# Layer 3 of a four-layer graph network: the second half of the attention score as one more projection column

## The chip, the cores and the metric

The kernel runs on one core of a Trainium2 chip. The metric is the device time of one execution in microseconds. Before the change it was 2033.64 us, the median of three runs (2031.97 to 2036.11).

A core has five engines that work side by side, each on its own stream of instructions: TensorE (PE in the profile; its weight loads are PEld), VectorE (DVE), ScalarE (ACT), GpSimd (POOL) and SyncE (SP), which here issues DMAs. They meet at semaphores.

## What is computed

Four graph layers with residual connections run on 128 graphs of 64 nodes with 256 features. The change lies in the last one, a graph attention:

```python
def _L3_gnn_ref(h, adj_matrix, W, a):
    Wh = jnp.einsum('bnf,fo->bno', h, W)
    a1, a2 = (a[:Fout, 0], a[Fout:, 0])
    s1 = Wh @ a1
    s2 = Wh @ a2
    e = s1[:, :, None] + s2[:, None, :]
    e = jnp.where(e >= 0, e, ALPHA * e)
    e = jnp.where(adj_matrix[None] == 0, -jnp.inf, e)
    attention = jax.nn.softmax(e, axis=-1)
    h_prime = jnp.einsum('bij,bjo->bio', attention, Wh)
    return h_prime
...
h = jnp.maximum(_layernorm(x, axis=-1), 0.0)
x = x + _L3_gnn_ref(h, adj, L3_gnn_W, L3_gnn_a)
```

A score is the sum of two halves: s1 of the row's node i and s2 of the column's node j. Both are linear in the features, so s2 = h (W a2).

## The kernel before

**Tiling.** The 8192 tokens go through layer 3 in 16 chunks of 512. A chunk is four tiles of 128 tokens, and a tile holds two graphs of 64 nodes, one in partitions 0 to 63, the other in 64 to 127. Everything is in 32-bit floats; an ordinary product of TensorE appears as two instructions in the trace, a transpose as one.

**The loop.** The pass n of the loop at L2005 works on several chunks at different stages:

- `second_norm(n + 2)` (L1852): TensorE transposes `o` (the output of layer 2, scaled) back to tokens, eight transposes at L1860; VectorE adds the residual (L1865, 128x1024) and takes the statistics (L1869, L1870); from chunk 3 on GpSimd makes the root of the variance and the shift (L1879 to L1882) and the normalised `h`, four instructions at L1886.
- `scale_o(n + 4)` (L1841): GpSimd scales layer 2's output into `o`, two instructions at L1848.
- `features(n + 1)` (L1894): eight transposes of `h` (L1901), then ScalarE applies the ReLU on its way to `hT` (L1904).
- `project3(n)` (L1910): for each tile two products of `hT` with `wext`, the 256 columns of W and one column W a1, 257 columns; ScalarE copies the bank to `wh` (L1925).
- `turn(n - 1)` (L1955): four transposes of the exponentials (L1960), copied by VectorE and ScalarE into `field` (L1964).
- `dense_scores(n)` (L1927): s2 of the chunk, spread over the rows, is made on TensorE from `hT` with `wa2`, in which the vector W a2 stands 64 times; four products with 64 columns of weights. VectorE adds s1, the column 256 of `wh` (L1937), applies the leaky ReLU (L1943), adds the mask (L1944) and takes the maximum (L1946); ScalarE makes the exponentials (L1949).
- `dense_values(n - 1)` (L1968): four products of `field` with `wh` (L51, "wh,field"), which VectorE scales and adds to the residual (L1975).

**The order.** The kernel is written in this program order, and a scheduler places the instructions of each engine's stream by its own cost model, except those marked with `late`, which stay in program order. In layer 3 few are marked, so an edit can move other instructions on every engine. `bank()` takes one of four PSUM banks, `pair_bank()` one of two double banks. `mm` (L51) records every product, so the profile gives L51 for `wext`, `wa2` and `wh` alike; they are told apart by the operands.

**Tables.** `late_tables` (L188 on) fills `wext` and `wa2` in layer 0's stage, among them `eye` (the 64x64 unit matrix, twice) in a pool that is freed afterwards.

Of the kernel before, what the change touches and what calls it, by code (L numbers as in the profile page):

```python
# [9 lines left out]
F32 = mybir.dt.float32  # L10
# [4 lines left out]
ALU = mybir.AluOpType  # L15
AX = mybir.AxisListType

P = 128
T = 64
D = 256  # L20
# [11 lines left out]
def gnn_stack_kernel(ctx: ExitStack, tc: tile.TileContext, a: dict, out: bass.AP):  # L32
    nc = tc.nc
# [10 lines left out]
    def bank():  # L44
        return psums["now"].tile([P, 512], F32, tag="bank", name="bank", bufs=psums["banks"])
# [4 lines left out]
    def mm(o, lhsT, rhs, start=True, stop=True):  # L50
        nc.tensor.matmul(o, lhsT, rhs, start=start, stop=stop)  # L51
# [20 lines left out]
    def late(ins):  # L72

        tc.keep_in_program_order(ins)
# [106 lines left out]

    tab2 = ctx.enter_context(tc.tile_pool(name="tab2", bufs=1))
    bdH = tab2.tile([P, P], F32, tag="bdH", name="bdH")
    wext = tab2.tile([P, 2, D + 1], F32, tag="wext", name="wext")
    wa2 = tab2.tile([P, 2, T], F32, tag="wa2", name="wa2")
    mask3 = tab2.tile([P, T], F32, tag="mask3", name="mask3")

    def late_tables():  # L188
        with ExitStack() as setup:
            s2 = setup.enter_context(tc.tile_pool(name="s2", bufs=1, side="right"))  # L190
            nc.sync.dma_start(out=wext[:, :, :D], in_=a["W3"])
            w3T = s2.tile([P, 2, D], F32, tag="w3T", name="w3T")
            nc.sync.dma_start(out=w3T, in_=a["W3T"])
            a3 = s2.tile([P, 2, 2], F32, tag="a3", name="a3")
            nc.sync.dma_start(out=a3, in_=a["a3"])

            late(nc.vector.tensor_scalar(mask3, adj2, 0.0, NEG, ALU.is_equal, ALU.mult))
            yield

            eye = s2.tile([P, T], F32, tag="eye", name="eye")  # L200
            for h in range(2):
                r = slice(h * T, (h + 1) * T)
                nc.vector.tensor_copy(eye[r, :], ident[r, r])
            an = s2.tile([P, T], F32, tag="an", name="an")
            anT = s2.tile([P, T], F32, tag="anT", name="anT")
            nc.vector.tensor_tensor(an, adj2, eye, ALU.add)
            nc.vector.tensor_tensor(anT, adjT2, eye, ALU.add)
            yield
            deg = s2.tile([P, 3], F32, tag="deg", name="deg")
            diag = s2.tile([P, T], F32, tag="diag", name="diag")  # L210
            nc.vector.tensor_tensor(diag, an, eye, ALU.mult)
            nc.vector.tensor_reduce(deg[:, 0:1], anT, AX.X, ALU.add)
            nc.vector.tensor_reduce(deg[:, 1:2], an, AX.X, ALU.add)
            nc.vector.tensor_reduce(deg[:, 2:3], diag, AX.X, ALU.add)
            yield
            dinv = s2.tile([P, 1], F32, tag="dinv", name="dinv")
            nc.vector.tensor_tensor(dinv, deg[:, 0:1], deg[:, 1:2], ALU.add)
            nc.vector.tensor_tensor(dinv, dinv, deg[:, 2:3], ALU.subtract)
            nc.gpsimd.tensor_tensor(dinv, dinv, half_power[:, 0:1], ALU.pow)
            yield  # L220
            dinv_b = s2.tile([P, P], F32, tag="dinv_b", name="dinv_b")
            nc.vector.tensor_copy(dinv_b, dinv.to_broadcast([P, P]))
            nc.vector.memset(bdH, 0.0)
            nc.vector.tensor_scalar(anT, anT, dinv, None, ALU.mult)
            yield
            p = bank()
            mm(p[:, :T], dinv_b[:T, :], ident[:T, :T])
            yield
            for h in range(2):
                r = slice(h * T, (h + 1) * T)  # L230
                nc.vector.tensor_tensor(bdH[r, r], p[r, :T], anT[r, :], ALU.mult)
            yield

            p = bank()
            for c in range(2):
                for k in range(2):
                    mm(
                        p[:, 2 * c : 2 * c + 2],
                        w3T[:, k, c * P : (c + 1) * P],
                        a3[:, k, :],  # L240
                        k == 0,
                        k == 1,
                    )
            yield
            for c in range(2):
                nc.vector.tensor_copy(wext[:, c, D:], p[:, 2 * c : 2 * c + 1])
                nc.vector.tensor_copy(wa2[:, c, :], p[:, 2 * c + 1 : 2 * c + 2].to_broadcast([P, T]))
            yield


# [195 lines left out]
    with ExitStack() as l0:  # L446
# [39 lines left out]
        with ExitStack() as conv:  # L486
# [38 lines left out]
            for h in range(2):  # L525
                r = slice(h * T, (h + 1) * T)
# [3 lines left out]
            p = bank()  # L530
# [4 lines left out]
            def graph_convolutions(n):  # L535
# [53 lines left out]
                if n >= NCH // 2:  # L589
                    nc.sync.dma_start(out=hmem[n], in_=dst)  # L590

            tables = chain(edge_tables(), late_tables())
            under_way = []
            for n in range(NCH + 4):
# [265 lines left out]
        for slot in range(len(tasks) + 2):  # L860
# [24 lines left out]
            if new:  # L885
                next(one)
                flight.append((new, one))
                at, k = new[0], new[2]
# [6 lines left out]
                if step.w == MAX_SKIP and step.t == 2 and k < 2 and step.g < NGR - 1:  # L895
                    for u in range(2):
                        n = 4 * step.g + 2 * u + k
                        later.append((slot, "x", n))
            while later and later[0][0] <= slot:
                _, kind, n = later.pop(0)  # L900
# [27 lines left out]
    with ExitStack() as l1:  # L928
# [32 lines left out]
        for g, c in last_outs:  # L961
            for u in range(2):
                n = 4 * g + 2 * u + c
# [482 lines left out]
    with ExitStack() as l2:  # L1446
        def pool2(name, bufs):
            return l2.enter_context(tc.tile_pool(name=name, bufs=bufs, reuse_waits="tile"))
# [53 lines left out]
        with ExitStack() as dense2:  # L1502
# [67 lines left out]
            with ExitStack() as first_dense:  # L1570
# [43 lines left out]
                for slot, (pr, m2) in enumerate(tasks):  # L1614
                    n = slot + 3
# [128 lines left out]
        t4 = pool2("t4", 2)  # L1744
# [9 lines left out]
        xts, norms, hT3, att3 = {}, {}, {}, {}  # L1754
# [155 lines left out]
        def project3(n, tiles):  # L1910

            if n not in att3:
                wh = t4.tile([P, 4, D + 1], F32, tag="wh", name="wh", bufs=3)
                att3[n] = [wh, None, None]
            for i in tiles:
                p = bank()
                for k in range(2):
                    mm(
                        p[:, : D + 1],
                        hT3[n][:, k, i * P : (i + 1) * P],  # L1920
                        wext[:, k, :],
                        k == 0,
                        k == 1,
                    )
                nc.scalar.copy(att3[n][0][:, i, :], p[:, : D + 1])  # L1925

        def dense_scores(n):  # L1927

            wh, hT = att3[n][0], hT3.pop(n)

            p = bank()
            for k in range(2):
                hv = hT[:, k, :].rearrange("p (i o t) -> p o i t", o=2, t=T)
                for h in range(2):
                    mm(p[h * T : (h + 1) * T, : 4 * T], wa2[:, k, :], hv[:, h], k == 0, k == 1)
            e = t4.tile([P, 4, T], F32, tag="e3", name="e3")
            nc.vector.tensor_tensor(  # L1937
                e,
                p[:, : 4 * T].rearrange("p (i t) -> p i t", t=T),
                wh[:, :, D:].to_broadcast([P, 4, T]),  # L1940
                ALU.add,
            )
            nc.vector.scalar_tensor_tensor(e, e, 0.2, e, ALU.mult, ALU.max)  # L1943
            nc.vector.tensor_tensor(e, e, mask3.unsqueeze(1).to_broadcast([P, 4, T]), ALU.add)  # L1944
            nmx = stat.tile([P, 4], F32, tag="nmx3", name="nmx3")
            nc.vector.tensor_reduce(nmx, e, AX.X, ALU.max, negate=True)  # L1946
            den = stat.tile([P, 4], F32, tag="den3", name="den3")
            for i in range(4):
                nc.scalar.activation(  # L1949
                    e[:, i, :], e[:, i, :], AF.Exp, bias=nmx[:, i : i + 1], accum_out=den[:, i : i + 1]  # L1950
                )
            nc.vector.reciprocal(den, den)
            att3[n][1:] = [e, den]
# [45 lines left out]
        for _ in start:  # L1999
            pass  # L2000
        project3(0, (0, 1))
        for _ in second:
            pass
        scale_o(3)
        for n in range(NCH + 1):  # L2005
            if 4 <= n + 4 < NCH:
                fetch(n + 4)
            if n + 2 < NCH:
                for _ in second_norm(n + 2):
                    pass  # L2010
            if n + 4 < NCH:
                scale_o(n + 4)
            if n == 0:
                project3(0, (2, 3))
                dense_scores(0)
                features(1)
                continue
            if n + 1 < NCH:
                features(n + 1)
            if 0 <= n < NCH:  # L2020
                project3(n, (0, 1))
            if n >= 1:
                turn(n - 1)
            if 0 <= n < NCH:
                project3(n, (2, 3))
                dense_scores(n)
            if n >= 1:
                dense_values(n - 1)
# [68 lines left out]
```

## Time and profile before

| what | us |
|---|---|
| median of three runs | 2033.64 |
| the profiled execution | 2017.19 |
| its span, first to last instruction | 2015.0 |
| TensorE busy | 1963.0 |
| VectorE busy | 1245.3 |
| ScalarE busy | 1160.6 |
| GpSimd busy | 365.1 |
| products with wa2, 128 instructions | 17.3 |
| layer 3, first o transpose to the end of the span | 1860.7 to 2015.0 |

The busy times are of the profiled execution, whose own time is below the median of the other runs. Lines of a timeline give the start in us from the span's start, the busy time, the engine, the line, the operation with output and inputs, the number of instructions put together, and in brackets how long the engine had been idle and what ended that. Lines of a table by stretches give the length, then the busy time and the number of instructions of TensorE, its weight loads, VectorE, ScalarE and GpSimd, then the granted TensorE clock as a share of full speed, the DMA share and GB/s. Lines of a group give the number of instructions, their busy time and the mean of one in ns.

### The profile page before, as it was taken

Reading aid. Unit: us, or ns where it says so; the run is one execution under the profiler, and the core shown is the slowest. Engines: PE = TensorE matmul, PEld = TensorE weight load, DVE = VectorE, ACT = ScalarE, POOL = GpSimd, SP = SyncE. Lnnn points to the kernel's source line nnn. Section 1 sums busy time; section 2 is a strip of 40 time slices with the busy share of each in tenths; the row PEclk is TensorE's granted clock in tenths of the full one; section 3 lists DMA queues with packets and bytes.
Section 4 is the critical chain, followed back from the end, with each engine's and each line's share of the span. In section 5 each row is a group of like instructions: output and inputs, shape, how many; then the busy total and the mean of one; then the engine's idle time right before and its main releaser. Section 6 shows DMA issues by size and latency. Waiting matters only on the chain. (4 is left out here: it accounts for less than half of the span.)

```text
span 2015.0 us, 26089 instructions
## 1 busy us (share of the span) xinstructions
PE 1963.0 (97%) x9720; PEld 1395.9 (69%) x9720; DVE 1245.3 (62%) x2418; ACT 1160.6 (58%) x2177; POOL 365.1 (18%) x534
## 2 busy tenths in 40 slices
PE   7999999999999999999999999999999999999998
PEld 5777468866678864888666888666566875444786
DVE  8774675575475567665645655534444877886776
ACT  4343775565465547665555555577776556691544
POOL 3000031030030011310300200213223420000563
PEclk9999999999999999999999999999999999999999
DMA  8422000010010053001001000621334841022012
GB/s 289 134 76 87 0 22 1 0 42 0 1 42 1 1 189 103 21 1 42 1 0 42 1 0 25 204 92 58 126 110 141 300 147 53 0 84 84 32 63 74
DMA packets 63486, 135.62 MB, mean 67 GB/s; under 512 B 6272, under 2 KB 40960, under 8 KB 61056
## 3 DMA queue, kind: packets, MB, share of 16 engines
q1 hardware_dynamic: 57120, 109.65, 16.2%
q0 software_dynamic: 5632, 24.12, 3.2%
q8 instruction: 76, 1.25, 0.3%
q14 instruction: 50, 0.41, 0.1%
q10 hardware_dynamic: 608, 0.20, 0.0%
HBM read 87.54 MB, written 46.40 MB: 66 GB/s over the span
## 5 line engine op out<-in xcount | busy, mean ns | idle before, releaser
L719 ACT ACTIVATE gate<-gate,bias 128x256 f32<-128x256 f32 (+2 forms) x368 | 247.2, 678 | 180.6 <-DVE gate L735 99.6
L691 PE MATMUL pa<-xop,sih 128*128 128x256 f32 (+2 forms) x1056 | 342.4, 417 | 8.9 <-DVE gate L745 8.7
L691 PEld LDWEIGHTS pa<-xop,sih 128*128 128x128 f32 x1056 | 199.0, 190 | 82.9 <-issue 21.8
L691 PE MATMUL pc<-xop,wih 128*128 128x256 f32 (+2 forms) x736 | 251.1, 423 | 0.0
L735 DVE TENSOR_TENSOR gate<-pb,gate 128x256 f32<-128x256 f32 (+2 forms) x184 | 87.4, 475 | 226.5 <-PE pb L691 150.5
L691 PE MATMUL pa<-lstm_h,shh 128*128 128x256 f32 (+1 forms) x672 | 212.7, 398 | 0.0
L691 PEld LDWEIGHTS pc<-xop,wih 128*128 128x128 f32 x736 | 139.8, 190 | 51.2 <-issue 23.0
L750 DVE TENSOR_TENSOR gate<-pc,gate 128x256 f32<-128x256 f32 (+2 forms) x184 | 87.6, 476 | 112.8 <-PE pc L691 112.6
L691 PEld LDWEIGHTS pa<-lstm_h,shh 128*128 128x128 f32 x672 | 127.7, 190 | 30.2
L1057 ACT ACTIVATE lr<-pair 128x1024 f32<-128x1024 f32 x128 | 123.7, 1018 | 34.9 <-PE pair L1047 33.3
L691 PE MATMUL pc<-lstm_h,whh 128*128 128x256 f32 (+1 forms) x448 | 141.8, 398 | 0.0
L734 ACT COPY gate<-pa 128x256 f32<-128x256 f32 (+2 forms) x184 | 76.1, 413 | 95.3 <-PE pa L691 94.9
L745 DVE TENSOR_TENSOR gate<-pa,gate 128x256 f32<-128x256 f32 (+2 forms) x184 | 87.4, 475 | 43.9 <-PE pa L691 43.3
L1018 PE MATMUL bank<-wlv,hT 128*128 128x260 f32 x480 | 112.9, 387 | 0.4
L1027 DVE TENSOR_TENSOR xq<-bank,xq 128x260 fp32r<-128x260 f32 x64 | 27.1, 428 | 138.9 <-ACT xq L1026 138.9
L719 ACT ACTIVATE gate<-pa,bias 128x256 f32<-128x256 f32 (+2 forms) x184 | 93.8, 510 | 31.2 <-PE pa L691 29.8
L739 ACT COPY gate<-pa 128x256 f32<-128x256 f32 (+2 forms) x184 | 75.2, 409 | 53.1 <-PE pa L691 52.1
L1018 PEld LDWEIGHTS bank<-wlv,hT 128*128 128x128 f32 x480 | 88.5, 190 | 22.9 <-issue 9.1
L691 PE MATMUL pa<-xop,wih 128*128 128x256 f32 (+1 forms) x320 | 101.6, 399 | 2.8 <-ACT xop L672 2.7
L691 PE MATMUL pb<-xop,wih 128*128 128x256 f32 (+1 forms) x320 | 100.4, 398 | 0.0
L691 PEld LDWEIGHTS pc<-lstm_h,whh 128*128 128x128 f32 x448 | 85.1, 190 | 20.1
L742 ACT COPY gate<-pc 128x256 f32<-128x256 f32 (+2 forms) x136 | 57.9, 426 | 52.5 <-PE pc L691 51.9
(366 smaller groups left out, 3842.5 us busy)
## 6 DMA issues: line engine op xcount, KB each, us to landing
field<-keep SPq DMA_DIRECT2D x4, 2304.0 KB, 13.2
wih<-in_WihT SPq DMA_DIRECT2D x8, 1024.0 KB, 7.1
xres<-in_x SPq DMA_DIRECT2D x16, 512.0 KB, 4.6
xa<-xres POOLq DMA_DIRECT2D x16, 512.0 KB, 4.1
dense<-field POOLq DMA_DIRECT2D x4, 2048.0 KB, 10.0
xin<-xb SPq DMA_DIRECT2D x16, 512.0 KB, 3.7
h<-xb SPq DMA_DIRECT2D x16, 512.0 KB, 3.6
xin<-in_x SPq DMA_DIRECT2D x15, 512.0 KB, 5.1
```

Source lines behind the costliest of these rows:

```text
L691: ins = nc.tensor.matmul(p[:, : self.N], weights[kind, self.phase](k, q), x[k], start=first_ and kind == "ih", stop=kind == "hh" or not se ...
L719: nc.scalar.activation(out, in_, AF.Tanh if q == 2 else AF.Sigmoid, bias=bias[:, self.w - 1, 2 * q + j : 2 * q + j + 1],)
L734: nc.scalar.copy(blk[0, 0], pa[:, :N])
L735: nc.vector.tensor_tensor(blk[0, 0], pb[:, :N], blk[0, 0], ALU.add)
L739: nc.scalar.copy(blk[1, 0], pa[:, :N])
L742: (nc.vector.tensor_copy if not self.t and self.w > 1 else nc.scalar.copy)(blk[1, 1], pc[:, :N])
L745: nc.vector.tensor_tensor(blk[1, 1], pa[:, :N], blk[1, 1], ALU.add)
L750: nc.vector.tensor_tensor(blk[1, 0], pc[:, :N], blk[1, 0], ALU.add)
L1018: ins = nc.tensor.matmul(o, hTs[n][:, k, i * P : (i + 1) * P], wlv[:, k, cols], start=k == 0, stop=k == 1)
L1027: nc.vector.tensor_tensor(xq[:, 1, :], p[:, :QS], xq[:, 0, :].bitcast(F32), ALU.subtract)
L1057: nc.scalar.activation(lr, p, AF.Relu)
```

## The change

`wext` gets a second extra column, W a2, so `project3` computes s2 for each node along with the rest, in 258 columns. `dense_scores` then has s2 with one node in each partition and needs it along the row. GpSimd multiplies each s2 with a row of `eye`, which gives `across`: in row j only column j is not zero. One product with `same_graph`, which is one where both nodes are in the same graph, sums over the nodes of a graph and so writes s2 of every node j into every row. This stands in place of the four products with `wa2`. `eye` moves into a pool that stays.

```diff
-    wext = tab2.tile([P, 2, D + 1], F32, tag="wext", name="wext")
-    wa2 = tab2.tile([P, 2, T], F32, tag="wa2", name="wa2")
+    wext = tab2.tile([P, 2, D + 2], F32, tag="wext", name="wext")
+    same_graph = tab2.tile([P, P], F32, tag="same_graph", name="same_graph")
+    eye = tab2.tile([P, T], F32, tag="eye", name="eye")
...
-            eye = s2.tile([P, T], F32, tag="eye", name="eye")
+            nc.vector.memset(same_graph, 0.0)
             for h in range(2):
                 r = slice(h * T, (h + 1) * T)
                 nc.vector.tensor_copy(eye[r, :], ident[r, r])
+                nc.vector.memset(same_graph[r, r], 1.0)
...
             for c in range(2):
-                nc.vector.tensor_copy(wext[:, c, D:], p[:, 2 * c : 2 * c + 1])
-                nc.vector.tensor_copy(wa2[:, c, :], p[:, 2 * c + 1 : 2 * c + 2].to_broadcast([P, T]))
+                nc.vector.tensor_copy(wext[:, c, D:], p[:, 2 * c : 2 * c + 2])
...
-                wh = t4.tile([P, 4, D + 1], F32, tag="wh", name="wh", bufs=3)
+                wh = t4.tile([P, 4, D + 2], F32, tag="wh", name="wh", bufs=3)
...
                     mm(
-                        p[:, : D + 1],
+                        p[:, : D + 2],
                         hT3[n][:, k, i * P : (i + 1) * P],
                         wext[:, k, :],
                         k == 0,
                         k == 1,
                     )
-                nc.scalar.copy(att3[n][0][:, i, :], p[:, : D + 1])
+                nc.scalar.copy(att3[n][0][:, i, :], p[:, : D + 2])
...
         def dense_scores(n):
-            wh, hT = att3[n][0], hT3.pop(n)
-
+            wh = att3[n][0]
+            hT3.pop(n)
+            across = t4.tile([P, 4, T], F32, tag="across", name="across")
+            nc.gpsimd.tensor_tensor(
+                across,
+                wh[:, :, D + 1 :].to_broadcast([P, 4, T]),
+                eye.unsqueeze(1).to_broadcast([P, 4, T]),
+                ALU.mult,
+            )
             p = bank()
-            for k in range(2):
-                hv = hT[:, k, :].rearrange("p (i o t) -> p o i t", o=2, t=T)
-                for h in range(2):
-                    mm(p[h * T : (h + 1) * T, : 4 * T], wa2[:, k, :], hv[:, h], k == 0, k == 1)
+            mm(p[:, : 4 * T], same_graph, across.rearrange("p i t -> p (i t)"))
...
-                wh[:, :, D:].to_broadcast([P, 4, T]),
+                wh[:, :, D : D + 1].to_broadcast([P, 4, T]),
                 ALU.add,
             )
```

## The prediction

> **What bounds the kernel now.** I read the page first (which engine is full), then the stage in windows (is it full there too), then the timeline of one round (what each queue holds, and when). A round is one pass n of the loop at L2005; there are sixteen, one for each chunk of 512 tokens, and the change touches nothing else that lies on a long path.
>
> ```profile
> span 2015.0 us, 26089 instructions
> PE 1963.0 (97%) x9720; PEld 1395.9 (69%) x9720; DVE 1245.3 (62%) x2418; ACT 1160.6 (58%) x2177; POOL 365.1 (18%) x534
> ```
>
> ```profile
> 1920.00:1940.00 20.00, 20.00 (x122) 16.38 (x121) 16.33 (x45) 9.74 (x37) 14.39 (x25) 1.00 0.16 53
> ```
>
> In this stage too TensorE (first column after the stretch) is never idle, while GpSimd (the fifth) is busy 14.39 of 20 us, four times its mean share. So product time saved counts in full here, but only while nothing makes TensorE wait, and GpSimd has little room. The timeline shows where:
>
> ```profile
> 1926.49 0.23 POOL L1879 TENSOR_SCALAR ln_rs<-ln_mv 128x4 f32<-128x4 f32 x1 [2.44 <-DVE ln_mv L1870]
> 1926.86 1.08 PE L51 MATMUL bank<-hT,wa 128*64 128x256 f32 x8
> 1927.88 2.00 PE L51 MATMUL pair<-wh,field 128*128 128x256 f32 x8
> ...
> 1928.54 2.61 POOL L1886 TENSOR_SCALAR h<-h,ln_rs,ln_nm 128x256 f32<-128x256 f32 x4
> ...
> 1929.71 1.04 PE L1860 MATMUL pair<-ident,o 128*128 128x128 f32 x8
> ...
> 1931.13 1.52 POOL L1848 TENSOR_SCALAR o<-h,scale,shift 128x512 f32<-128x512 f32 x2
> ...
> 1931.76 1.21 DVE L1865 TENSOR_TENSOR h<-pair,h 128x1024 f32<-128x1024 f32 x1
> 1931.89 1.04 PE L1901 MATMUL pair<-ident,h 128*128 128x128 f32 x8
> ```
>
> The score products (hT,wa) start at 1926.86 in this round and at 1935.47 in the next, so a round is 8.61 us. GpSimd's block (root, four h tiles, two o tiles) runs from 1926.49 to 1931.13 + 1.52 = 1932.65, 6.16 us, and starts at almost the same moment as the score products. It waits 2.44 us for VectorE's statistics before it.
>
> **Removed and added on TensorE.** Per round eight wa instructions go, 1927.88 - 1926.86 = 1.02 us. The product with the graph ones is one product of 256 columns, two instructions; the four of wh,field take 1929.71 - 1927.88 = 1.83, so one takes 0.46. The extra column costs sixteen instructions x 1 of 257 columns, 0.01. Net 0.55 us a round, 8.8 in sixteen, if TensorE stays full.
>
> **Added around it.** The product now waits for a new GpSimd instruction (across), which waits for ScalarE's copy of the last tile. Its price is in no row. The nearest rows are two-input products of 128x256 on GpSimd:
>
> ```profile
> L680 POOL TENSOR_TENSOR xop<-xop 128x256 f32<-128x256 f32 x10 | 15.9, 1592 | 0.8
> ...
> L137 POOL TENSOR_TENSOR w1S<-w1T,w1S 128x256 f32<-128x256 f32 x1 | 0.7, 747 | 0.0
> ```
>
> Bounds 0.72 and 1.59 us; the lower rows are dense in shape and run beside a less loaded VectorE, so I take 0.8. From the last projection, across alone needs 0.1 + 0.37 (copy) + 0.1 + 0.8 + 0.1 = 1.5 us.
>
> **Where the queues hold it.** This decides. In the built streams of the changed kernel, across(n) stands on GpSimd behind root(n+2), four h(n+2) and two o(n+4), that is, behind the 6.16 us block that today starts with the score products; and in front of root(n+3). On TensorE the ones product of round n stands two or four wh,field products after the last projection (in every second round also half of the o transposes), and in front of the o transposes of chunk n+3, all or half. Their streams around a round of kind A, cut to these lines:
>
> ```
> GpSimd:  root(n+2) x4, h(n+2) x4, o(n+4) x2, across(n), root(n+3) ...
> TensorE: wext x4, wh,field x4, o-transposes(n+3) x4, ones product(n), o-transposes(n+3) x4, wext(n+1) ...
> VectorE: L1975, scores, L1975, L1943, L1865, L1944, statistic, maximum, statistics ...
> ```
>
> In the trace each engine's instructions come in the order of its stream, so there is a ring from one ones product to the next: o transposes(n+3) -> L1865 and statistics on VectorE -> root, h(n+3), o(n+5) on GpSimd -> across(n+1) -> ones product(n+1) -> o transposes(n+4). Today TensorE does not wait in it, since the score products need no GpSimd. What is queued behind the waiting product is the rest of wh,field and all transposes; VectorE waits for both, and GpSimd for VectorE.
>
> Length of the ring, from rows of this timeline (pace from start to start). Rounds with half of the transposes already done (A): product and handover 0.63; on VectorE scores 0.46, one L1975 0.45, L1943 0.46, then L1865 1.24, L1944 0.46, maximum 0.45, statistics 1.70 (2.01 less the field copy): 5.85. Handover 0.09, GpSimd block 6.16, handover 0.1, across 0.73, handover 0.15: 13.1 us. Rounds with all transposes and two wh,field behind the product (B): 0.63, then four L1975 (1.76), scores, L1943, L1944, maximum (1.83) stand before L1865, 1.24, then reciprocal and statistics with the field copy 2.11: 7.57, and the same 7.23: 14.8. Against 8.61.
>
> The score products of rounds 0 to 13 are thirteen intervals, 1987.12 - 1875.06 = 112.06 us. After: round 0 to 1 13.2 (as A, with a reciprocal more); five B 74.0; five A 65.4; 11 to 12 without the o tiles 14.8 - 1.52 = 13.3; 12 to 13 one wh,field less again 12.8. Sum 178.7, so +66.6. The first product waits 1.45 for its chain (+1.5); after round 13 there is no block, and what is saved there (0.55 a round) goes into the exposed chain: 0.
>
> **Corrections.** VectorE will be idle while GpSimd works, and h then costs less: 1.09 for two, 0.545 each where VectorE was idle, against 0.653: -0.43 a round, -5.6. Across at 0.8 instead of 0.73: +0.9. And the clock:
>
> ```profile
> 1858.00:1860.00 2.00, 0.00 (x0) 0.00 (x0) 1.84 (x8) 0.30 (x1) 0.00 (x0) 0.83 0.62 223
> ...
> 1870.00:1872.00 2.00, 2.00 (x7) 1.49 (x6) 0.00 (x0) 0.38 (x2) 0.00 (x0) 0.50 0.00 0
> 1872.00:1874.00 2.00, 2.00 (x12) 1.92 (x11) 0.92 (x3) 1.51 (x4) 0.87 (x2) 0.76 0.00 0
> ```
>
> At the stage's start TensorE has a gap of 4.0 us; the granted clock (third figure from the end) falls to half within it, 2.7 us in, and stays there until 1873.0, 5.8 us after TensorE became steadily busy. A round has 8.0 us of TensorE work, so the gaps will be 3 to 6 us. In a round that starts at half clock the first handover grows by 0.45, and in B the field copy, which stands before the last statistic, comes 0.85 later still: +0.45 (A), +1.3 (B), +11.8 if all thirteen rounds start so. Since a slow start fills part of the next gap I take half, +5.9.
>
> The Trainium skill, "TensorE: Matmul & The Clock Gate", Part 1, What's actually happening, puts the fall at an idle window of about 3.4 us and the recovery at about 3.4 us busy, on a free-running window. The fall here agrees roughly, the recovery at 5.8 us was slower; by the page's recovery my estimate is that the cold rounds lose about half as much, some 3 us less in the sum.
>
> Sum: 66.6 + 1.5 - 5.6 + 0.9 + 5.9 = +69.3, rounded to +70. In the profiled execution 2017.19 becomes 2087; the median of the runs lies 16.4 higher, and the difference is carried to it: 2033.64 + 70 = **2104 us**. Its own ends: no clock loss, +63 (2097); all rounds cold, h not faster and across at 1.59, 66.6 + 1.5 + 11.8 + 14 x 0.86 = +92 (2126).
>
> The tables cost nothing: two memsets of graph ones on VectorE (128x128 took 0.165 us at L65) lie before the first data arrive; bare, 0.4. wa's two copies go, 0.3 at most, in a stage that TensorE fills. No DMA is added or moved; SP's stream is the same.
>
> **Rivals.**
> - Faster, on the other side: the ones product waits only for its own chain. That would be so if GpSimd's block were done by the last projection; then 8.8 is gained less 0.6 in the B rounds (1.5 needed, 0.91 covered): -4 to -9, 2025 to 2030. For it: the saving is real and TensorE is full. Against: the block would have to start 6 us earlier than at 1926.49, and VectorE's statistics end just there. It decides once across is queued ahead of root and h. Chance 0.05.
> - No change: that gain is eaten by a later exponential, whose transposes already wait at the end (2006.02): 2030 to 2037. Chance 0.03.
> - Slower still: the clock stays at half through whole rounds. TensorE's 8.0 us become 15.8 (eight projection instructions took 3.59 at half, 1.83 at full), more than the ring: 13 x 15.8 - 112 = +93 and more, 2127 to 2140. For it: the gaps return each round. Against: each round begins with over 5.8 us of steady work. Chance 0.09.
>
> The forecast has 0.83. **Range** 2085 to 2130: the forecast's own ends, some room below for a ring shorter than rows say, and the lower edge of the third rival. Faster by over 0.2% (4 us, about what a measurement here can tell) 0.05, same 0.03, slower 0.92.
>
> **What would show it.** Right: ones products 13 to 15 us apart; TensorE idle before them with across as releaser, in total some 60 us; across starting within 0.1 us of the last o tile; the last slices of TensorE at 5 to 7 tenths, their clock under 1. Step by step: a ones product near 0.46, across near 0.8, the block 5.7 to 6.2. Wrong: across starting long before the o tiles end, rounds under 9 us, or TensorE waiting for VectorE's exponential input rather than for GpSimd.

## The result and the profile after

The changed kernel takes 2093.61 us (median of six runs, 2090.16 to 2095.92) against 2032.81 for the kernel before (six runs on the same chip): a ratio of 1.0295, 95% interval 1.028 to 1.031, so some 60 us slower. 2104 was predicted, in a range of 2085 to 2130.

The profiled execution took 2090.16. The page, its first lines, TensorE's busy slices with the granted clock, and the chain of work that ended last:

```profile
span 2088.4 us, 25890 instructions
PE 1985.4 (95%) x9624; PEld 1409.1 (67%) x9624; DVE 1238.7 (59%) x2419; ACT 1158.3 (55%) x2177; POOL 370.9 (18%) x550
...
PE   7999999999999999999999999999999999997777
...
PEclk9999999999999999999999999999999999998998
...
POOL 4%; DVE 3%; PE 1%; issue 1%; ACT 0%; DVEq 0%; POOLq 0%; ACTq 0%
```

TensorE issues 96 instructions fewer, and is busy for longer. The loss sits in the last four slices of 40, which are layer 3; the chain that sets the end now runs over GpSimd and VectorE, where that of the kernel before ran mostly over TensorE:

```profile
PE 22%; DVE 3%; ACT 1%; issue 1%; POOL 0%; POOLq 0%; DVEq 0%; ACTq 0%
```

In the 167.0 us of the thirteen intervals between the score products (a stretch of the windows view, columns as before, TensorE first, GpSimd fifth, then the clock), beside the 112.0 us of the kernel before:

```profile
1890.00:2057.00 167.00, 124.59 (x597) 97.15 (x597) 82.21 (x249) 57.53 (x201) 76.86 (x144) 0.91 0.11 38
```

```profile
1875.00:1987.00 112.00, 111.41 (x677) 89.58 (x676) 87.79 (x253) 58.74 (x201) 71.42 (x125) 1.00 0.17 57
```

TensorE was full and is now idle for 42 of 167 us. The view of waits of the changed kernel (who waited for whom, us in total, times, longest) tells what for:

```profile
POOL ln_rs L1880 <- DVE ln_mv L1871: 81.4, 12, 8.5
...
DVE e L1942 <- PE bank L51: 53.4, 13, 6.3
...
PE bank L51 <- POOL across L1933: 32.2, 14, 3.7
```

Three engines wait for one another in a circle: GpSimd's root for VectorE's statistics, VectorE's scores for TensorE's product, TensorE's product for GpSimd's across. No single share of busy time shows that. The timeline of one round shows the circle (changed kernel; line numbers are one to five above those of before):

```profile
1928.61 0.70 PE L51 MATMUL bank<-across,same_graph 128*128 128x256 f32 x2 [1.50 <-POOL across L1933]
...
1932.45 1.22 DVE L1866 TENSOR_TENSOR h<-pair,h 128x1024 f32<-128x1024 f32 x1
...
1935.54 0.16 DVE L1871 BATCH_NORM_AGGREGATE ln_mv<-ln_st 128x2 f32<-128x6 f32 x1
1935.80 0.23 POOL L1880 TENSOR_SCALAR ln_rs<-ln_mv 128x4 f32<-128x4 f32 x1 [7.25 <-DVE ln_mv L1871]
...
1937.85 2.17 POOL L1887 TENSOR_SCALAR h<-h,ln_rs,ln_nm 128x256 f32<-128x256 f32 x4
...
1940.00 1.52 POOL L1849 TENSOR_SCALAR o<-h,scale,shift 128x512 f32<-128x512 f32 x2
1941.48 0.62 POOL L1933 TENSOR_TENSOR across<-wh,eye 128x256 f32<-128x256 f32 x1
1942.15 1.22 PE L51 MATMUL bank<-across,same_graph 128*128 128x256 f32 x2 [3.61 <-POOL across L1933]
```

From 1928.61 every row waits for the one above it, VectorE's rows through its queue, which it works off from the scores at 1929.41 without a pause: 7.09 us until VectorE's last statistic ends, 0.10 of handover, 5.68 for GpSimd's block, 0.62 for across, 0.05, and the next product starts after 13.54 us. The thirteen intervals are 12.95, 13.55, 11.87, 13.54, 12.39, 13.62, 11.87, 13.63, 12.39, 13.62, 12.17, 12.13 and 13.32. Their sum is 167.05 against 112.06 before, +55.0. From the start of layer 3 (the first o transpose) to the first product +1.3, from the fourteenth product to the end +3.2: +59.5 in all, which agrees with the medians. (The spans differ by 73.4, since the profiled execution of before was quicker than its other runs; its layer 3 began 14 us earlier.)

### The profile page after: what moved, and what is told of

Same layout as the page of the kernel before. It is cut to its first block, busy times and chain, and to the rows that moved or that the text cites. A ratio compares the mean times of both kernels' runs of the same rounds, so it can differ in the third digit from the quotient of the medians.

```text
span 2088.4 us, 25890 instructions
## 1 busy us (share of the span) xinstructions
PE 1985.4 (95%) x9624; PEld 1409.1 (67%) x9624; DVE 1238.7 (59%) x2419; ACT 1158.3 (55%) x2177; POOL 370.9 (18%) x550
## 5 line engine op out<-in xcount | busy, mean ns | idle before, releaser
L1048 PE MATMUL pair<-sd_hot,xq 64*128 64x512 f32 x512 | 80.0, 428 | 7.4 <-ACT lr L1058 6.4
```

The lines of the kernel that those rows point to most:

```text
L1048: ins = nc.tensor.matmul(p[:, par, :], queries[it][r, piece, c * P : (c + 1) * P], sd_hot[r, :], start=piece == 0, stop=piece == 1,)
```

## The experiments

Each kernel was timed against the kernel before on the same chip. That kernel's own median was 2030.29, 2017.22 and 2031.04 us in the three groups of runs, so the ratios are what compares. "First" is from layer 3's first o transpose to the first score product, "loop" the thirteen intervals, "tail" the rest, all in us from the profiles.

| kernel | ratio to before, 95% | first | loop | steady round | tail |
|---|---|---|---|---|---|
| before | 1 | 14.4 | 112.1 | 8.61 | 27.9 |
| changed | 1.0295 (1.028 to 1.031) | 15.7 | 167.1 | 11.87 to 13.6 | 31.1 |
| across unread | 0.9957 (0.9943 to 0.997) | 14.5 | 103.6 | 7.84 | 26.6 |
| across ahead of the block | 1.0074 (1.005 to 1.0097) | 20.7 | 112.8 | 8.68 | 31.9 |
| across on VectorE | 1.0018 (1.0001 to 1.0034) | 15.0 | 112.0 | 8.44 | 30.6 |
| values first | 1.0256 (1.0229 to 1.0284) | 15.2 | 160.0 | 11.97 to 13.3 | 31.5 |
| changed, h doubled | 1.0331 (1.0314 to 1.0348) | 15.7 | 172.2 | 12.9 and 14.1 | 31.9 |
| before, h doubled | 1.0006 (0.9996 to 1.0016) | 13.7 | 112.1 | 8.61 | 29.9 |
| VectorE, values first | 1.0118 (1.0101 to 1.0135) | 15.0 | 131.0 | 9.92 | 32.1 |
| VectorE, split | 1.0012 (1.0003 to 1.0022) | 15.3 | 112.9 | 8.44 | 30.6 |
| o on ScalarE | 1.0299 (1.0284 to 1.0314) | 18.8 | 164.4 | 12.05 to 13.4 | 30.4 |
| VectorE, h transposes first | 0.9981 (0.9968 to 0.9993) | 14.6 | 107.5 | 8.15 | 29.3 |
| the same, split | 0.997 (0.9958 to 0.9981) | 14.8 | 104.7 | 7.84 | 27.9 |

### The wait alone taken away

```diff
-            mm(p[:, : 4 * T], same_graph, across.rearrange("p i t -> p (i t)"))
+            mm(
+                p[:, : 4 * T].rearrange("p (i t) -> p i t", t=T),
+                same_graph,
+                eye.unsqueeze(1).to_broadcast([P, 4, T]),
+            )
```

> The ones product reads the constant eye matrix (four copies side by side) in place of across, so the second score half is left out of the result. GpSimd still computes across in every round, in the same place of its order (after root, four h, two o), but nothing reads it. GpSimd does the same work as in the changed kernel; only TensorE's wait for it is gone. Ring theory (the time comes from the product waiting for across behind the block, which itself waits for what the product released): the loop is cut, rounds fall back to about 8.1 us (8.61 before less 0.55 saved on TensorE), so the time is about 2033 - 8.8 = 2024, range 2020 to 2034. Rival 'load' (0.62 us more GpSimd work per round, contention with VectorE, later h): the time stays above 2070, product intervals stay at 12 to 13.6 us. Rival 'clock' (the half clock after idle spells is most of the +61): follows the ring theory here, since the idle spells go.

Measured: 0.9957, 2021.08 against 2030.29, -9.2 us. One round of its timeline:

```profile
1934.48 0.61 POOL L1933 TENSOR_TENSOR across<-wh,eye 128x256 f32<-128x256 f32 x1
...
1936.43 0.23 POOL L1880 TENSOR_SCALAR ln_rs<-ln_mv 128x4 f32<-128x4 f32 x1 [1.33 <-DVE ln_mv L1871]
...
1936.77 0.59 PE L51 MATMUL bank<-eye,same_graph 128*128 128x256 f32 x2
1937.20 1.89 PE L51 MATMUL pair<-wh,field 128*128 128x256 f32 x8
```

GpSimd has exactly the instructions that it has in the changed kernel; the product has no bracket, so TensorE did not wait for it, and rounds are 7.84 us. Eleven of the thirteen intervals are 7.83 or 7.84. So GpSimd's added work costs nothing by itself; the price is the wait alone. (TensorE's stream moves a little with it: all four values products then follow the product in every round.)

### The queue alone changed

```diff
-                nc.gpsimd.tensor_scalar(rs, mv[:, :, 1], 1e-5, None, ALU.add)
+                late(nc.gpsimd.tensor_scalar(rs, mv[:, :, 1], 1e-5, None, ALU.add))
...
-            nc.gpsimd.tensor_tensor(
+            late(nc.gpsimd.tensor_tensor(
                 across,
...
+            if n >= 1:
+                rest()
```

Here `rest()` runs the second half of `second_norm(n + 2)` (root, h) and `scale_o(n + 4)` at the end of the pass instead of at its beginning; `late` keeps across ahead of them on GpSimd.

> All work is kept. On GpSimd across(n) now stands ahead of the block (root, four h, two o) of the next tile instead of behind it; TensorE's product stands after two values products in every round, the eight o transposes behind it. Ring theory: across then waits only for the last wh copy; the block that follows is hidden in a round, so rounds are 8.1 to 8.9 us and the time is 2024 to 2042 (own chain copy, across 0.62, product against 0.9 of two values products: up to 0.5 us a round of waiting, 13 x 0.5 = 6.5 on top of 2024, less or more by what h comes later). Rival 'own chain' (copy on ScalarE, then a GpSimd instruction with its start and semaphore, then the product is the expensive part, wherever GpSimd stands): still 2080 to 2095, intervals 12 or more, TensorE idle 3.6 us before the product. Rival 'load': also above 2070.

Measured: 1.0074, 2044.28, two us above the range that was given. Its steady rounds are 8.68 us:

```profile
1940.95 0.62 POOL L1933 TENSOR_TENSOR across<-wh,eye 128x256 f32<-128x256 f32 x1 [1.98 <-ACT wh L1926]
...
1941.62 0.70 PE L51 MATMUL bank<-across,same_graph 128*128 128x256 f32 x2
1941.66 0.23 POOL L1880 TENSOR_SCALAR ln_rs<-ln_mv 128x4 f32<-128x4 f32 x1
```

Across now waits for ScalarE's copy and for nothing else, and the block starts behind it, at the moment of the product. With the same instruction on the same engine the loop falls from 167.1 to 112.8 us. The rival "own chain" is refuted. What is left over is at the ends: in the first round the block still stood ahead of across in program order (first 20.7 instead of 15.7), and the tail is 4.0 longer than in the kernel before.

### Across on VectorE

```diff
-            nc.gpsimd.tensor_tensor(
+            nc.vector.tensor_tensor(
                 across,
```

> across is computed by VectorE instead of GpSimd; nothing else is moved by hand. VectorE's order has it after the statistics of the tile before, ahead of the scores. Ring theory: the block of GpSimd no longer stands in the loop; what is left is copy, across on VectorE (about 0.5 to 0.6 by its 128x256 rows), product against two values products of cover: 0 to 0.5 us of wait per round, so 2024 to 2036. Rival 'own chain' (the spread and its two handovers cost wherever they run): above 2060. Rival: VectorE itself becomes the bound through 0.6 more per round (its busy share in layer 3 of before leaves over 1 us per round): 2035 to 2050, with VectorE as the releaser of the scores' waits.

Measured: 1.0018, 2034.54; across took 0.42 us there, and rounds are 8.44. The ring is gone by this road as well. But 8.44 is 0.6 above what TensorE can do (7.84); what holds it there comes below.

### More cover for the own chain, the queue left as it is

```diff
             if 0 <= n < NCH:
                 project3(n, (2, 3))
-                dense_scores(n)
             if n >= 1:
                 dense_values(n - 1)
+            if 0 <= n < NCH:
+                dense_scores(n)
```

> All work is kept and across stays on GpSimd behind the block; only TensorE's order changes: all four values products stand ahead of the ones product, then the eight o transposes, in every round. This gives the own chain 0.9 us more cover (1.8 in all), enough for copy plus 0.62 of across. Ring theory: the loop is unchanged, product, eight o transposes, VectorE's add and statistics, block 5.7, across 0.6, product: about 13.6 less 0.9 for the two values products that no longer stand in it = 12.7 us a round, 13 x 12.7 = 165 against 167 measured: 2088 to 2096. Rival 'own chain': its wait is covered, so the stall goes: 2024 to 2035.

Measured: 1.0256, 2080.12, about 8 us below the range given for the ring theory and 45 above the rival's. The ring stays, but it is shorter than I worked out:

```profile
1924.41 0.70 PE L51 MATMUL bank<-across,same_graph 128*128 128x256 f32 x2 [1.47 <-POOL across L1933]
...
1930.00 0.23 POOL L1880 TENSOR_SCALAR ln_rs<-ln_mv 128x4 f32<-128x4 f32 x1 [5.64 <-DVE ln_mv L1871]
```

From the product to root are 5.59 us, against 7.19 in the round of the changed kernel shown above. I had taken only TensorE's two values products out of the ring; VectorE's four scalings of the values (1.66 us) left it too, since they are now done while TensorE waits. 5.59, and 6.38 for the block, across and handovers, make 11.97, the shortest of the steady intervals there (the last two, with no o tiles left to scale, are 10.5).

### One GpSimd instruction more, in both kernels

```diff
-            for i in range(4):
+            for i in (0, 1, 2, 3) if n < 3 else (0, 0, 1, 2, 3):
                 if n > 2 or i > 1:
```

> The changed kernel with the first of the four h instructions on GpSimd issued a second time in every round from tile 3 on (same values, nothing left out): the block grows by one 128x256 instruction, 0.54 to 0.58 us. TensorE's order shifts a little (in every other round the product stands after three or four values products and five o transposes instead of four). Ring theory: each of the 13 rounds grows by 0.54, less up to 0.2 from the shifted order: +4 to +8 on the changed kernel, so a ratio to before of 1.031 to 1.035 (2094 to 2101 with before at 2031). Rival (GpSimd's block is not what the product ends up waiting for; the wh copies or VectorE come last): no change against the changed kernel, ratio 1.028 to 1.031.

> The kernel before with the same doubled h instruction. Ring theory: GpSimd has over 2 us of idle time per round there and nothing waits for it in a loop, so 0 to +2 us: 2029 to 2034. Rival (GpSimd's block is already near the bound of a round in before, so that any addition to GpSimd costs): +0.55 x 13 = +7, 2036 to 2042.

Measured: 1.0331 for the changed kernel and 1.0006 for the kernel before, whose loop is 112.06 us as without it. In the changed kernel the intervals go from 13.62 to 14.11 in every second round, and from 12.39 (those that start at half clock) to 12.92 in the others:

```profile
1926.89 2.70 POOL L1887 TENSOR_SCALAR h<-h,ln_rs,ln_nm 128x256 f32<-128x256 f32 x5
1929.57 1.52 POOL L1849 TENSOR_SCALAR o<-h,scale,shift 128x512 f32<-128x512 f32 x2
1931.05 0.62 POOL L1933 TENSOR_TENSOR across<-wh,eye 128x256 f32<-128x256 f32 x1
1931.72 1.22 PE L51 MATMUL bank<-across,same_graph 128*128 128x256 f32 x2 [4.03 <-POOL across L1933]
```

The fifth h makes 2.70 of 2.17, +0.53, and a round grows by 0.49 to 0.53. Not all thirteen can be set side by side: one of 15.53 holds a spell at half clock (1916.6 to 1920.0), and at the end TensorE's order is another (the last is 9.56 instead of 13.32). In all the loop grew by 5.1 us, within the 4 to 8 expected. The same instruction is free before and counts in full in the rounds that compare: GpSimd's block was off the path and is on it now.

### The block shortened

```diff
-                late(nc.gpsimd.tensor_scalar(
-                    o[:, c, :], v[:, half[c], :], scale2[:, c : c + 1], shift2[:, c : c + 1], ALU.mult, ALU.add
+                late(nc.scalar.activation(
+                    o[:, c, :], v[:, half[c], :], AF.Identity, bias=shift2[:, c : c + 1], scale=scale2[:, c : c + 1]
```

> The changed kernel with the two o instructions of every tile moved from GpSimd to ScalarE, so that the block ahead of across shrinks by 1.5 us; across stays on GpSimd behind root and h. TensorE's order becomes the same in all rounds: two values products, product, two values products, eight o transposes (the longer kind, 13.6 us, instead of 13.6 and 12.0 by turns). Ring theory: 13 rounds of 13.6 - 1.5 = 12.1 instead of a mean of 12.85, -0.75 x 13 = -10: ratio 1.022 to 1.027. Rival (the o instructions run beside something else in the loop, ScalarE's copies come late): no change or slower, 1.029 or more.

Measured: 1.0299, as slow as the changed kernel. A miss, with the mechanism in it all the same:

```profile
1929.76 0.70 PE L51 MATMUL bank<-across,same_graph 128*128 128x256 f32 x2 [2.42 <-POOL across L1933]
...
1936.94 0.23 POOL L1880 TENSOR_SCALAR ln_rs<-ln_mv 128x4 f32<-128x4 f32 x1 [7.24 <-DVE ln_mv L1871]
...
1941.13 0.62 POOL L1933 TENSOR_TENSOR across<-wh,eye 128x256 f32<-128x256 f32 x1
1941.81 0.78 PE L51 MATMUL bank<-across,same_graph 128*128 128x256 f32 x2 [2.69 <-POOL across L1933]
```

This interval is 12.05, that is 13.54 less the 1.5 us of the two o instructions, as expected. But only five of thirteen were that short (12.05 to 12.22); the other eight are 12.66 to 13.40. In the trace each of these eight holds one spell of 3.41 us at half clock, and none of the five does. Against 12.1 the eight are 7.0 us longer in all, which is about what is missing: the loop gained 2.7 us and not 10. ScalarE's four o instructions at the start of the stage (2.93 us from 1873.60), ahead of the first norm's, took back about 3. The time lies where the rival had it, but the clock is not a reason that the rival gave.

### A version that beats both

With across on VectorE, what holds rounds at 8.44? Two experiments asked. In the first, the four values products were put ahead of the product, for cover; in the second, across was split so that its last piece is short:

> across on VectorE, and all four values products ahead of the ones product, so 1.8 us of TensorE work cover the chain copy, across 0.42, product (1.2 us). Ring theory: with the block out of the loop and the own chain covered, TensorE runs without a gap as with the unread across, 7.83 to 8.0 us a round; the last rounds keep 3 to 4 us of own chain: 2021 to 2028, so faster than before. Rival (the later product makes the exponents late for the turn, or VectorE with 0.42 more per round becomes the bound): rounds of 8.4 or more, 2030 to 2042.

> across on VectorE in two instructions, tiles 0 to 2 and then tile 3 alone, so that only a 128x64 instruction stands between the last wh copy and the product. Ring theory with the own chain as the rest: the wait shrinks by 0.2 to 0.3 us against across in one piece (rounds of 8.45): 8.15 to 8.3 us a round, 2028 to 2033. Rival (VectorE takes the first part late, or the split costs as much as it saves): 2033 to 2037.

Measured: 1.0118 and 1.0012. Both missed: more cover made it slower (9.92 us a round), and a shorter chain changed nothing (8.44). The first one's timeline names another circle:

```profile
1933.41 0.30 PE L1965 MATMUL bank<-ident,e 128*64 128x128 f32 x1 [1.59 <-ACT e L1954]
...
1935.82 1.99 PE L51 MATMUL pair<-wh,field 128*128 128x256 f32 x8
...
1937.66 0.59 PE L51 MATMUL bank<-across,same_graph 128*128 128x256 f32 x2
1937.91 1.66 DVE L1980 SCALAR_TENSOR_TENSOR h<-pair,den,h 128x256 f32<-128x256 f32 x4 [1.17 <-PE pair L51]
...
1939.49 0.41 DVE L1942 TENSOR_TENSOR e<-bank,wh 128x256 f32<-128x256 f32 x1
```

TensorE waits for the exponentials, transposes them, and their field is what the values products read. With values products ahead of the ones product, product -> scores -> exponentials -> turn -> field -> values -> next product closes. Here the scores stand moreover behind VectorE's four scalings, which wait for the values (1.17 us), so the circle closes by this way too.

The same circle, shorter, holds the rounds at 8.44, since with across on VectorE (in one piece or two) two values products stand ahead of the product:

```profile
1926.90 0.59 PE L51 MATMUL bank<-across,same_graph 128*128 128x256 f32 x2
...
1927.53 0.42 DVE L1942 TENSOR_TENSOR e<-bank,wh 128x256 f32<-128x256 f32 x1 [0.80 <-PE bank L51]
...
1933.49 0.38 DVE L1969 COPY field<-bank 64x256 f32<-64x256 f32 x1
...
1933.96 0.36 ACT L1969 COPY field<-bank 64x256 f32<-64x256 f32 x1 [0.24 <-DVE ln_mv L1871]
...
1934.37 1.13 PE L51 MATMUL pair<-wh,field 128*128 128x256 f32 x4 [0.19 <-ACT field L1969]
...
1935.34 0.59 PE L51 MATMUL bank<-across,same_graph 128*128 128x256 f32 x2
```

From 1927.53 VectorE works off its queue without a pause until its half of the field is copied at 1933.87; ScalarE's half follows, then two values products, and the next product starts 8.44 us after the last. The chain over across, which the split shortened, is not in this circle.

In the kernel before and in the first experiment the product stands ahead of the values, which leaves the circle open. So the product needs cover that depends neither on GpSimd's block nor on the field: the eight h transposes of the next tile.

```diff
-            if n + 1 < NCH:
-                features(n + 1)
             if 0 <= n < NCH:
                 project3(n, (0, 1))
...
                 project3(n, (2, 3))
+            if n + 1 < NCH:
+                features(n + 1)
+            if 0 <= n < NCH:
                 dense_scores(n)
```

> All work is kept. across on VectorE in one piece, and the eight h transposes of the next tile stand between the last projections and the ones product in every round (0.87 us of TensorE work as cover); the four values products follow the product, as in the kernel before. So the product is behind neither the block nor the values (with the product behind the values, the loop product, scores, exponents, turn, field, values closes on itself, 8.45 to 9.9 us). Ring theory: rounds between the gapless 7.83 and 8.3 us, 13 x 0.3 to 0.8 = 4 to 10 us less than before in the loop, 3 to 4 us more in the first and last rounds: a ratio to before of 0.997 to 1.000. Rival (another loop closes, exponents late for the turn, or VectorE): rounds of 8.5 or more, ratio above 1.001.

> As the kernel with h transposes ahead of the product, but across on VectorE in two pieces (tiles 0 to 2, then tile 3), and TensorE's order has one values product ahead of the ones product: cover 1.1 us against a chain of about 1.0. Ring theory: rounds of 7.85 to 8.2 us, ratio 0.996 to 0.9995. Rival (one values product ahead of the product is enough to close the loop over the field, or the second VectorE instruction costs what it saves): rounds of 8.4 or more, ratio 1.000 to 1.003.

Measured: 0.9981 (0.9968 to 0.9993) and 0.997 (0.9958 to 0.9981; 2024.13 against 2031.04 us), so both are below both kernels; against the kernel before it is by 0.2 and 0.3 per cent only, with intervals that leave out 1. The second, 20 us of its stage and the product in it:

```profile
1940.00:1960.00 20.00, 20.00 (x120) 17.69 (x119) 17.62 (x57) 11.13 (x42) 13.49 (x25) 1.00 0.24 80
```

```profile
1936.11 0.18 DVE L1935 TENSOR_TENSOR across<-wh,eye 128x64 f32<-128x64 f32 x1
...
1936.66 0.59 PE L51 MATMUL bank<-across,same_graph 128*128 128x256 f32 x2
```

TensorE is full again at full clock, and its rounds are 7.84, as in the kernel in which nothing was waited for. The h transposes and one values product stood ahead of the product there; that one did not close the circle. Its loop is 7.4 us shorter than before.

## Why the prediction was right

**The ring, and where it comes from: right, and shown.** It was read from the built streams and the timeline of the kernel before. Cutting the read (across unread), the place in the queue (across ahead of the block) or the engine (VectorE) each brings the loop to 104 to 113 us; giving the own chain cover does not; and a GpSimd instruction that is free before counts in full after, in the rounds that compare.

**The faster rival** (the product waits only for its own chain) gave its condition: across queued ahead of root and h. That condition was made, and the loop fell to 112.8, which is that of before. Its gain of 4 to 9 us did not come with it, because two values products stand ahead of the product there, as with across on VectorE: TensorE waits for the field before them (eight times between 1900 and 1990, 1.6 us). It came in the last version.

**Length of the ring: 0.87 us too long per round.** With the corrections for h and across (-0.43 and +0.07) the prediction has 12.74 and 14.44 for kinds A and B at full clock; measured are 11.87 and some 13.6, so seven of the thirteen intervals lie under the 13 to 15 us that it gave as a sign. Block 5.73 after correction, measured 5.68: right. Across at 0.8, 0.62. From across to the product 0.15, 0.05; from the o tiles to across 0.1, nothing. On VectorE from product to last statistic 7.57, 7.09; several instructions there start 0.33 to 0.40 after the one ahead, not 0.45 as I took from the kernel before; why, I did not trace. (L1944 was not even 0.45 there: its rows show 0.66, and with that the ring would have been predicted 0.2 longer still.) Thirteen rounds at 0.87 make 11.3 us too much; with the -1.9, -0.2 and +3.2 that follow the sum is -10.2, against 9.8 between the +69.3 predicted and the +59.5 measured.

**The clock: some 4 instead of 5.9.** Each of the five rounds of kind A holds a spell at half clock, after a gap of 3.6 us. In two the clock had fallen before the product, which took 1.22 instead of 0.70, and the interval is 12.39 instead of 11.87; in a third it fell during the product (1.01, interval 12.17). In the other two it fell 0.6 and 0.8 us after the product's start, about when VectorE began on the scores; it then ran without a pause (1968.97 to 1973.58 in one of them), so the ring lost nothing. Rounds of kind B, whose gap before them was 1.50 us or less, start at full clock. That makes 1.3 us. By what the first and the last interval are longer than the prediction less 0.87, they lost 1.0 and 1.7; I put that down to the clock, since both hold a spell (from 1897.0 and from 2043.8), but it is a remainder and not measured. To take half of the worst case was a guess that fell near.

**First product, +1.5:** +1.3. **After round 13, 0:** +3.2. This term failed. The timeline of the changed kernel's last values, then that of the kernel before:

```profile
2077.44 1.42 PE L1965 MATMUL bank<-ident,e 128*64 128x128 f32 x4 [2.23 <-ACT e L1954]
2079.76 3.78 PE L51 MATMUL pair<-wh,field 128*128 128x256 f32 x8 [0.90 <-ACT field L1969]
```

```profile
2006.02 1.29 PE L1960 MATMUL bank<-ident,e 128*64 128x128 f32 x4 [0.57 <-ACT e L1949]
2008.22 2.00 PE L51 MATMUL pair<-wh,field 128*128 128x256 f32 x8 [0.90 <-ACT field L1964]
```

In the last round two values products have moved ahead of the product and no longer fill the wait for the exponentials, 2.23 instead of 0.57; after this gap the last eight values instructions run at half pace, 3.78 instead of 2.00. I had argued that what is saved there goes into the chain, and had not asked what the gap does to the clock.

**TensorE idle for across, about 60 us: 32.2.** The step that failed is taking the excess of a round for idle time. TensorE's work in thirteen rounds is 13 x 7.84 = 102 us in the kernel without waits, but it was busy for 124.6: some 23 us of the waiting show as busy time, of which the mean clock of 0.91 explains 15 at most; the rest I did not trace. In the thirteen intervals TensorE was idle for 42 us: 31.7 of the 32.2 for across and 10.6 at other waits, 7.9 of them for exponentials at the turn.

**Saved on TensorE, 0.55 a round: right as a size.** Without waits a round is 0.77 shorter; the product itself takes 0.43 (1936.77 to 1937.20) against 1.02, 0.59. The rest I did not trace.

## What to carry to other kernels

Before work is moved to an engine that is half idle, look at what its queue holds at that moment and what that block waits for: if it waits for something that stands behind the new consumer, a ring closes, and its length, not any engine's busy time, sets the pace. To tell the ring from the price of the new instruction, keep the instruction and let its consumer read a constant. When cover is sought for a new chain, use work that is in no circle with the consumer: here more of the wrong cover cost 20 us, and as much of the right one turned a loss into a gain.

## What the runs showed of the hardware

- A GpSimd product of two broadcast inputs, 128x256, took 0.617 to 0.621 us in all sixteen rounds, below all the rows that bounded it (0.717 to 1.592); the same on VectorE, in the kernel with across there, took 0.43 as a median, 0.90 at most. The Trainium skill, "GPSIMD Engine Reference", section 3.1, has 4.50 us on GpSimd and 2.29 on VectorE for a sum of 2048 elements per partition; my estimate from its figures, an eighth, is 0.56 and 0.29, where an instruction's fixed part is divided too, and the runs lie 0.06 and 0.14 above. Where the rows of a trace are far apart, such a page can say which of them is the odd one.
- GpSimd's h instructions took 2.17 us for four in the changed kernel, in stretches where VectorE waits, and 2.31 to 2.62, mostly about 2.6, in the kernel before. In the kernel with across unread, where VectorE is busy beside them, they took 2.30.
- The granted clock changed only in steps of 3.41 us. In layer 3 of the changed kernel the spells at half clock last 3.41, 6.83 or 13.65 us up to the last one, which runs to the end, and from 1917.5 on those of the loop begin 7 or 8 steps apart (1917.5, 1941.4, 1968.7, 1992.6, 2019.9, 2043.8). Every gap of 3.6 us ahead of the product went with one; only the moment differed: the clock fell 0.7 us before the product of 1942.15, which took 1.22, and 0.6 us after the start of the one of 1968.16, which took 0.71.
- Whether a shorter gap costs clock depended on more than its length. In the kernel with the values first, the product from 1987.46 took 1.22 after an idle time of 2.41 us, at half clock, and the one from 2025.77 took 0.70 after 2.41 as well, at full clock. The Trainium skill, "TensorE: Matmul & The Clock Gate", Part 1, What's actually happening, says that the activity window is about 3.4 us long and runs freely. The steps of 3.41 us agree with that, and a gap's place among them would then decide; how much of a window must be idle, no run here settles.
